# Two norm tiles a unit, their add one step behind, and conjugates ahead of the products

## The chip, the cores and the metric

The kernel runs on one core of one Trainium2 chip. The metric is the device time of the program in microseconds (us); a run's profile also gives the span of the program's instructions on the core. The engines go on independently, each in the order in which its instructions were written, and wait for each other by semaphores: TensorE (PE; its weight loads PEld), VectorE (DVE), ScalarE (ACT), GpSimd (POOL) and SyncE (SP), which here issues the DMA transfers.

## The reference

The input is x with shape (4, 128, 128, 128): 4 batches, 128 channels, an image of 128 x 128. Two layers follow each other.

The first layer treats the 16384 pixels of a batch as a sequence: an MLP, an input projection, a short causal convolution, a selective scan with 16 states for each of 256 channels, a gate and an output projection. Its output is normalised over 4 groups of channels, passed through silu, and x is added:

```python
g = (g - mu) * lax.rsqrt(var + EPS)
xn = jax.nn.silu(g.reshape(B, C, H, W) * gn_w[None, :, None, None] + gn_b[None, :, None, None])
return xn + x
```

The second layer takes that result as `features`. A group norm, a 1x1 convolution with relu and a mean over the image give, through a softmax, four weights per batch. These mix four complex filters, and the product of the spectrum with its filtered self is transformed back:

```python
xf = jnp.fft.rfft2(x32, norm='ortho')
wc = (filt_w[..., 0] + 1j * filt_w[..., 1]).astype(jnp.complex64)
filtered = jnp.fft.irfft2(xf[:, None] * wc[None], s=(h, w), norm='ortho')
ff = jnp.fft.rfft2(filtered, norm='ortho')
product = xf[:, None] * ff
weighted = jnp.sum(weights[:, :, None, None, None].astype(product.dtype) * product, axis=1)
out = jnp.fft.irfft2(weighted, s=(h, w), norm='ortho') + residual_weight * x32
```

## The kernel before

The kernel has two blocks, one after the other. `block0` is the first layer, in chunks of 512 pixels, all four batches; it also finishes the norm, the silu and the pooling of batches 0, 1 and 2 while the next batch is scanned (`finish`, called with its own step numbers). The pixels of a normed batch are written to DRAM as `x1`. `block1` is the spectral part for all batches, and it also has to finish batch 3.

**Units and steps of `block1`.** A unit is 8 channels of one batch: 8 images. There are 16 groups of channels times 4 batches, 64 units. Each unit has three blocks, of 3, 3 and 2 images, and the main loop runs one step `t` per block: unit `t // 3`, block `t % 3`. The work of a block is spread over later steps, so that a step holds work of several blocks. In a step the instructions are written in this order:

- at the first step of a unit, on SP: the filters of a channel group that are due (L736, four transfers of 520 KB) and the images of the next unit, `load(n + 1)` (L742, 512 KB);
- `over_h(t)`: PE transforms each image along its rows into the single PSUM bank `pa` (L776), ScalarE copies half of it to `sa` (L778);
- `evict(t - 8)`: VectorE moves `pz` from PSUM to `sz` (L835);
- `residual(t - 9)`: VectorE adds the last transform in `po` to the image times the residual weight (L848); after a unit's last block SP stores the result (L851);
- `products(t - 2)`: VectorE forms the real and imaginary part of the squared spectrum (L801, L802), then its two products with the mixed filter `wb` (L808, twice);
- `conjugates(t)`: VectorE fills the other half of `sa` from the same bank `pa` (L783);
- `over_w(t - 1)`: PE transforms `sa` into `px` (L790, L791; two banks), ScalarE makes a doubled copy and two squares of it, called xs below (L793 to L795);
- `back_h(t - 7)` and `back_w(t - 8)`: PE transforms back into `pz` (L829, L830; two banks) and `po` (L841; one bank);
- by `t % 3`: the filters of a unit times the batch's weights on ScalarE (`term`, L749: the fourth of this unit at the first step, the first two of the next unit at the second, its third at the third), their sum on POOL (`mix`, L755), on POOL the sums of the products (L815, L816), on ScalarE the mirrored halves (`copies`, L821, L822);
- last, the work of batch 3 that is due in this step, by the phases `pe`, `act`, `dve` and `end`.

The first term of a unit goes into the tile `wb`, of which there are two. It can be written only when the products of the unit two before it have been formed, the last of them in the second step of a unit.

**Batch 3.** `finish` returns a list of (step, phase, function). A norm tile is 512 pixels of all 128 channels; there are 32. `norm_load` issues two loads of 256 KB on SP (L561, L562); `norm_act` is the silu on ScalarE into the PSUM bank `pf` (L567), of which there is one; `norm_dve` adds x on VectorE (L571) and stores the tile to DRAM from SP (L572); `norm_stats` takes the statistics of the second norm on VectorE (L575). The function `norm` gives the steps of load, silu and add: for tile i they are 5 + i, 8 + i and 8 + i. After the last tile come the group statistics, then 32 pooling tiles, one a step (`agg_load`, `agg_mm` L597, `agg_act` L601), from step t1 = 54, then the softmax. The tags `xr` and `o` have four buffers each.

**The order of the units.** Units of batch 3 can't start before its weights are there. `spare` is the last step of `finish` in units; the groups of channels in `wait` are run for batches 0 to 2 first. Of these groups the last three keep their filters for batch 3; the others (`late`) load them once more for a single unit. Before the change `spare` is 33, there are 11 groups in `wait`, 8 of them late, and 5 groups with all four batches in a row.

**Names of stages.** Below, the norm stage is the steps with norm tiles (9 to 40 by the transforms), then a transition, the pooling stage (54 to 85), and the plain stage from 86 to the last step, 191.

Of the kernel before, what the change touches and what calls it, by code (L numbers as in the profile page):

```python
# [500 lines left out]
def group_norm(s, io, b, mat, which, stat, at, then):  # L501


    nc = s.nc
    g = {}

    def small(n, m=1):
        g[n] = io.small.tile([P, m], F32, tag=n, name=f"{n}_{which}_{b}")
        return g[n]

    def aggregate():
        nc.vector.bn_aggr(small("mv", 2), stat().rearrange("p n q -> p (n q)"))

    def mean_mm():
        ps = g["ps"] = io.psum(f"gm_{which}_{b}")
        nc.tensor.matmul(ps[:, 0:1], mat, g["mv"][:, 0:1], start=True, stop=True)

    def spread_act():
        mv = g["mv"]
        nc.scalar.copy(small("mean"), g["ps"][:, 0:1])  # L520
        q = small("q")
        nc.scalar.activation(q, mv[:, 0:1], AF.Square, scale=-1.0, bias=g["mean"])
        nc.scalar.activation(q, q, AF.Identity, bias=mv[:, 1:2])

    def var_mm():
        ps = g["ps"] = io.psum(f"gv_{which}_{b}")
        nc.tensor.matmul(ps[:, 0:1], mat, g["q"], start=True, stop=True)

    def root_act():
        nc.scalar.activation(small("rstd"), g["ps"][:, 0:1], AF.Sqrt, bias=s.eps)  # L530

    def invert():
        nc.vector.reciprocal(g["rstd"], g["rstd"])
        then(g["mean"], g["rstd"])

    return [
        (at, "dve", aggregate), (at, "end", mean_mm), (at + 1, "act", spread_act), (at + 3, "pe", var_mm),
        (at + 3, "act", root_act), (at + 3, "dve", invert),
    ]


def finish(s, io, b, first, norm, agg):

    nc, NCH, C, L, NF = s.nc, s.NCH, s.C, s.L, s.NF
# [86 lines left out]
    todo = group_norm(s, io, b, s.g0, 0, lambda: stats[b], first, start)  # L633
    for i in range(NCH):
        at = norm(i)
        todo += [
            (at[0], "pe", partial(norm_load, i)), (at[1], "act", partial(norm_act, i)),
            (at[2], "dve", partial(norm_dve, i)), (at[2], "end", partial(norm_stats, i)),
        ]
    c = at[2] + 5  # L640
    todo += group_norm(s, io, b, s.g1, 1, lambda: g["stat"], c, middle)
# [1 line left out]
    for i in range(NCH):  # L643
        at = agg(i)
# [11 lines left out]
def block1(tc, s):  # L656
# [7 lines left out]
    nc, B, C, H, W, WF, NF, NCH = s.nc, s.B, s.C, s.H, s.W, s.WF, s.NF, s.NCH  # L664
    HH = H // 2
    filt = s.a["filt_w"].rearrange("f c h w q -> h f c (w q)")
    with ExitStack() as ctx:
        def pool(name, bufs, **kw):
            return ctx.enter_context(tc.tile_pool(name=name, bufs=bufs, **kw))
# [10 lines left out]
        def const(name, shape):  # L680
# [14 lines left out]
        io = SimpleNamespace(  # L695
            big=pool("big", 4), bufs=4, small=small, psum=lambda n: psf.tile([P, T], F32, tag="pf", name=f"pf_{n}")
        )
        t1 = 8 + NCH + 14
        todo = defaultdict(list)
        steps = finish(s, io, B - 1, 0, lambda i: (5 + i, 8 + i, 8 + i), lambda i: (t1 + i - 3, t1 + i, t1 + i, None))  # L700
        for at, phase, f in steps:
            todo[at, phase].append(f)
        spare = max(at for at, _ in todo) // 3 + 2
# [23 lines left out]
        for k, ft in enumerate(spans):  # L727
            at = ft.first - 4
            if k >= KEEP:
                at = max(at, spans[k - KEEP].last)  # L730
            loads[max(at, 0)].append(ft)

        def load_filter(ft):
            ft.t = p2.tile([H, NF, CC, 2 * WF], F32, tag="ft", name=f"ft_{ft.first}", bufs=KEEP)
            for f in range(NF):
                nc.sync.dma_start(out=ft.t[:, f], in_=filt[:, f, ft.c0 : ft.c0 + CC, :])  # L736

        def load(n):
            if n < N:
                c0, b = units[n]  # L740
                u[n].xt = p2.tile([H, CC, W], F32, tag="xt1", name=f"xt1_{n}", bufs=6)
                nc.sync.dma_start(out=u[n].xt, in_=s.x1[b][c0 : c0 + CC].rearrange("c h w -> h c w"))  # L742

        def term(n, f):

            if 0 <= n < N:
                tag, bufs = ("term", 3) if f else ("wb", 2)
                t = p2.tile([H, CC, 2 * WF], F32, tag=tag, name=f"{tag}_{n}_{f}", bufs=bufs)
                nc.scalar.activation(t, u[n].ft.t[:, f], AF.Copy, scale=s.wts[units[n][1]][0:H, f : f + 1])  # L749
                u[n].terms = [t] if f == 0 else u[n].terms + [t]  # L750

        def mix(n, f):
            if 0 <= n < N:
                wb = u[n].terms[0]
                nc.gpsimd.tensor_tensor(wb, wb, u[n].terms[f], ALU.add)  # L755
# [16 lines left out]
        @block  # L772
        def over_h(e, n, m, k):
            e.pa = psa.tile([W, 3, 2, WF], F32, tag="pa", name=f"pa_{n}_{m}")
            for q in range(k):
                nc.tensor.matmul(images(e.pa)[:, q], u[n].xt[:, m + q, :], fh, start=True, stop=True)  # L776
            e.sa = p2.tile([W, 3, 2, H], F32, tag="sa", name=f"sa_{n}_{m}")
            nc.scalar.copy(e.sa[:, 0:k, :, 0:HH], e.pa[:, 0:k, :, 0:HH])  # L778

        @block  # L780
        def conjugates(e, n, m, k):
            o = e.sa[:, 0:k, :, HH:]
            nc.vector.tensor_tensor(o, e.pa[:, 0:k, :, 1:], sign.to_broadcast([W, k, 2, HH]), ALU.mult)  # L783
# [13 lines left out]
        @block  # L797
        def products(e, n, m, k):

            sq = psr.tile([H, 2, 3, WF], F32, tag="sq", name=f"sq_{n}_{m}")  # L800
            nc.vector.tensor_tensor(sq[:, 1, 0:k], e.px[:, 0:k, 0], e.xs[:, 1, 0:k], ALU.mult)  # L801
            nc.vector.tensor_tensor(sq[:, 0, 0:k], e.xs[:, 0, 0:k], e.px[:, 0:k, 1], ALU.subtract)  # L802
            if m == 0:
                u[n].p = [p2.tile([H, 2, CC, WF], F32, tag=f"pr{q}", name=f"pr{q}_{n}") for q in range(2)]
            wv = u[n].terms[0].rearrange("h c (k q) -> h q c k", q=2)
            for q in range(2):
                w = wv[:, q : q + 1, m : m + k, :].to_broadcast([H, 2, k, WF])
                nc.vector.tensor_tensor(u[n].p[q][:, :, m : m + k, :], sq[:, :, 0:k], w, ALU.mult)  # L808
# [23 lines left out]
        @block  # L832
        def evict(e, n, m, k):
            e.sz = p2.tile([W, 3, H], F32, tag="sz", name=f"sz_{n}_{m}")
            nc.vector.tensor_copy(e.sz[:, 0:k], e.pz[:, 0:k])  # L835

        @block
        def back_w(e, n, m, k):
            e.po = pso.tile([H, 3, W], F32, tag="po", name=f"po_{n}_{m}")
            for q in range(k):  # L840
                nc.tensor.matmul(e.po[:, q, :], e.sz[:, q, :], iw, start=True, stop=True)  # L841

        @block
        def residual(e, n, m, k):
            if m == 0:
                u[n].ot = p2.tile([H, CC, W], F32, tag="ot", name=f"ot_{n}")
            o, xt = u[n].ot[:, m : m + k], u[n].xt[:, m : m + k]
            nc.vector.scalar_tensor_tensor(o, xt, s.resw[0:H], e.po[:, 0:k], ALU.mult, ALU.add)  # L848
            if m + k == CC:
                c0, b = units[n]  # L850
                nc.sync.dma_start(out=s.out[b, c0 : c0 + CC].rearrange("c h w -> h c w"), in_=u[n].ot)  # L851

        with tc.manual_schedule():
            load(0)
            for t in range(3 * N + LAG + 3):
                n, i = divmod(t, 3)
                if i == 0:
                    for ft in loads[n]:
                        load_filter(ft)
                    load(n + 1)  # L860
                    if n == 0:
                        for f in range(NF):
                            term(0, f)
                            if f:
                                mix(0, f)
                over_h(t)
                evict(t - LAG - 1)
                residual(t - LAG - 2)
                products(t - 2)
                conjugates(t)  # L870
                over_w(t - 1)
                back_h(t - LAG)
                back_w(t - LAG - 1)
                if i == 0:
                    if n:
                        term(n, 3)
                        mix(n, 2)
                    copies(n - 2)
                elif i == 1:
                    term(n + 1, 0)  # L880
                    term(n + 1, 1)
                    if n:
                        mix(n, 3)
                else:
                    term(n + 1, 2)
                    sums(n - 1)
                    mix(n + 1, 1)
                for phase in ("pe", "act", "dve", "end"):
                    for f in todo[t, phase]:
                        f()  # L890
# [79 lines left out]
```

## Time and profile before

| | us |
|---|---|
| median of 3 runs | 7444.82 (7441.77 to 7446.32) |
| the profiled execution | 7446.74 |
| its span | 7445.0 |
| second block's first transform starts | 6626.55 |
| norm stage, first transform of step 9 to that of step 41 | 184.9 |
| transition, to step 54 | 49.9 |
| pooling stage, to step 86 | 141.7 |
| plain stage, to the transform of step 191 | 378.3 |

In the profile an engine's busy time is the union of its instructions. A line of instructions has start, duration, engine, source line, operation, output and inputs, their shapes and a count, and in brackets the idle time of the engine ahead of it with what ended it. A line of waits has the waiting instruction, the one that it waited for, the sum, the count and the longest. "Granted clock" is the share of its full clock that TensorE was given.

### The profile page before, as it was taken

The page shows a single profiled execution, that of the slowest core. Times are in us where ns is not written, and L with a number is a line of the kernel's source. Part 1 is how long each engine was busy: PE and PEld are TensorE (multiplying, and loading weights), DVE is VectorE, ACT ScalarE, POOL GpSimd, SP SyncE. Part 2 cuts the span into 40 slices and gives each one's busy share as a digit, 9 for nine tenths or more (in the row PEclk, how much of TensorE's full clock was granted, in tenths as well). Part 3 has the DMA queues.
Part 4 walks back from the last instruction along what each step waited for, and adds up shares of the span by engine and source line. Part 5 has one row for each costly group of instructions (what it writes and reads, how often), then busy time and mean ns, then how long its engine had stood idle before and what let it go on. Part 6 is the DMA issues. An engine that isn't in the chain of part 4 may idle for free.

```text
span 7445.0 us, 90541 instructions
## 1 busy us (share of the span) xinstructions
PE 6005.7 (81%) x25908; PEld 2664.1 (36%) x25908; DVE 7031.4 (94%) x8168; ACT 6328.6 (85%) x13181; POOL 6900.6 (93%) x3188
## 2 busy tenths in 40 slices
PE   7787878877778788887777788877777788867999
PEld 2223223322222233332222223232222233237999
DVE  6999999999999999999999999999999999977787
ACT  6888888888888888888888888888888888866887
POOL 6999999999999999999999999999999999976788
PEclk8888888888888888888888889988888889889999
DMA  4444444444554544544545454445554554547665
GB/s 138 159 154 150 151 156 156 143 161 168 174 188 164 179 165 156 169 166 169 184 168 185 161 171 166 159 165 175 171 188 166 173 169 151 173 149 216 177 185 155
DMA packets 853767, 1242.06 MB, mean 167 GB/s; under 512 B 76680, under 2 KB 308240, under 8 KB 853264
## 3 DMA queue, kind: packets, MB, share of 16 engines
q1 hardware_dynamic: 851152, 1236.11, 50.3%
q8 instruction: 204, 3.34, 0.2%
q14 instruction: 299, 2.45, 0.1%
q10 hardware_dynamic: 2112, 0.16, 0.0%
HBM read 992.71 MB, written 243.27 MB: 166 GB/s over the span
## 4 chain that ended last, share of the span: by engine, by line
ACT 20%; DVE 19%; PE 17%; POOL 9%; issue 8%; DMA 5%; SPq 1%; DVEq 0%; ACTq 0%; POOLq 0%
DVE da L409 8%; ACT da L391 8%; DVE h L409 6%; PE pp_cv L231 5%; ACT bt L299 4%; POOL hb L358 4%; POOL hb L416 4%; DVE hb L411 3%; DMA dd<-delta 2%; PE y L430 2%; PE pa L776 1%; ACT L391 1%; PE px L790 1%; PE px L791 1%; POOL du L307 1%
## 5 line engine op out<-in xcount | busy, mean ns | idle before, releaser
L358 POOL TENSOR_TENSOR hb<-rdu,rB 128x1536 f32<-128x1536 f32 (+2 forms) x1536 | 3607.6, 2365 | 16.2 <-DMA rdu<-dd 16.2
L416 POOL TENSOR_TENSOR hb<-h,rC 128x1024 f32<-128x1024 f32 (+1 forms) x1072 | 2438.7, 2277 | 279.8 <-DVE h L409 263.0
L391 ACT ACTIVATE da<-rdelta,amat 128x512 f32<-128x512 f32 x4096 | 2674.6, 696 | 9.2 <-ACT st L412 0.2
L409 DVE TENSOR_TENSOR_SCAN da<-da,st,hb 128x512 f32<-128x512 f32 x1976 | 2420.3, 1268 | 7.1 <-ACT da L391 7.0
L378 PE MATMUL b<-ident,bt 128*128 128x128 f32 x4096 | 768.9, 311 | 767.9 <-DVE h L409 633.0
L430 PE MATMUL y<-hb,sel 128*32 128x512 f32 x8192 | 1364.0, 743 | 4.8 <-POOL hb L416 2.9
L409 DVE TENSOR_TENSOR_SCAN h<-da,st,b 128x512 f32<-128x512 f32 x992 | 1261.3, 1271 | 111.4 <-POOL hb L358 37.5
L411 DVE TENSOR_TENSOR hb<-da,rC 128x512 f32<-128x512 f32 x2040 | 1296.7, 674 | 3.0
L409 DVE TENSOR_TENSOR_SCAN h<-da,st,hb 128x512 f32<-128x512 f32 x1000 | 1252.7, 1256 | 1.3 <-ACT da L391 1.3
L299 ACT ACTIVATE bt<-pt_dut,xdt 128x256 f32<-128x256 f32 x2048 | 1194.6, 708 | 46.8 <-PE pt_dut L288 46.5
L231 PE MATMUL pp_cv<-xm,wck 128*128 128x512 f32 x2048 | 1111.7, 692 | 9.8 <-ACT zs L225 9.7
L378 PEld LDWEIGHTS b<-ident,bt 128*128 128x128 f32 x4096 | 532.0, 156 | 1341.4 <-DVE h L409 997.1
L412 ACT COPY st<-da 128x1 f32<-128x1 f32 x2040 | 295.8, 173 | 567.9 <-DVE hb L411 562.6
L231 PEld LDWEIGHTS pp_cv<-xm,wck 128*128 128x128 f32 x2048 | 438.4, 226 | 771.1 <-issue 502.8
L755 POOL TENSOR_TENSOR wb<-wb,term 128x1040 f32<-128x1040 f32 x192 | 460.9, 2401 | 157.2 <-ACT term L749 147.2
L288 PE MATMUL pt_dut<-ident,du 128*128 128x128 f32 x1024 | 214.1, 337 | 280.5 <-ACT st L412 271.4
L426 PE MATMUL y<-u,diag 128*128 128x512 f32 x512 | 291.0, 651 | 156.8 <-DVE zs L440 155.6
L307 POOL TENSOR_TENSOR du<-delta,u 128x512 f32<-128x512 f32 x256 | 319.0, 1267 | 37.5 <-ACT delta L270 37.5
L417 ACT COPY st<-h 128x2 f32<-128x2 f32 (+1 forms) x1072 | 214.7, 200 | 162.8 <-DVE h L409 154.6
L288 PEld LDWEIGHTS pt_dut<-ident,du 128*128 128x128 f32 x1024 | 134.1, 164 | 578.6 <-POOL du L307 419.2
L196 PE MATMUL pp_h<-xt,w 128*128 128x512 f32 x512 | 296.6, 707 | 51.7 <-DMA xt<-in_x 46.6
L391 ACT ACT_TABLE_LOAD x261 | 334.9, 1283 | 2.9
(137 smaller groups left out, 8019.0 us busy)
## 6 DMA issues: line engine op xcount, KB each, us to landing
rdelta<-dd SPq DMA_DIRECT2D x1024, 256.0 KB, 3.6
rdu<-dd SPq DMA_DIRECT2D x1024, 256.0 KB, 4.6
rC<-bc SPq DMA_DIRECT2D x512, 256.0 KB, 5.1
rB<-bc SPq DMA_DIRECT2D x384, 256.0 KB, 3.5
dd<-delta SPq DMA_DIRECT2D x256, 256.0 KB, 5.3
dd<-du SPq DMA_DIRECT2D x256, 256.0 KB, 4.5
ft<-in_filt_w SPq DMA_DIRECT2D x96, 520.0 KB, 7.1
xt<-in_x SPq DMA_DIRECT2D x128, 256.0 KB, 5.5
```

The source lines that it names most:

```text
L231: nc.tensor.matmul(ps["cv", j], w, d["xm"][:, t : t + T], start=t == 0, stop=t == KC - 1)
L288: nc.tensor.transpose(ps["dut"][:, 2 * t + j, :], d["du"][:, j, at : at + P], s.ident)
L299: nc.scalar.activation(d["bt"][:, 2 * h + t, :, :, q], src, AF.Copy, scale=d["xdt"][:, 2 * h + t, R + q : R + q + 1])
L307: nc.gpsimd.tensor_tensor(du, d["delta"][:, j, :], d["u"][:, j, :], ALU.mult)
L358: nc.gpsimd.tensor_tensor(hb[:, p : p + n, :], d["du", j][:, m : m + n, :], d["B"][:, p - 1 : p - 1 + n, :], ALU.mult)
L378: nc.tensor.transpose(b[:, t * P : (t + 1) * P], src, s.ident)
L391: nc.scalar.activation(d["da", p][q], d["delta", j][:, m, :], AF.Exp, scale=s.amat[:, c : c + 1])
L409: nc.vector.tensor_tensor_scan(o, das[q], b, init, ALU.mult, ALU.add)
L411: nc.vector.tensor_tensor(hb[:, p + q, :], das[q], d["C"][:, p + q, :], ALU.mult)
L416: nc.gpsimd.tensor_tensor(hb[:, ps, :], h[:, q, :], d["C"][:, ps, :], ALU.mult)
L430: nc.tensor.matmul(y[m * DG : (m + 1) * DG, :], s.sel, d["hb", j, r][:, p, :], start=False, stop=r == NG - 1)
L755: nc.gpsimd.tensor_tensor(wb, wb, u[n].terms[f], ALU.add)
```

## The change

Three edits, all of them in the second block. In a step, VectorE's conjugates of block `t` are written ahead of the products of block `t - 2`. The add of a norm tile gets a phase of its own, "add", which is written right behind the products and in front of the column transform; it belongs to the step after its silu's. The statistics stay in the phase "end", at the step of the add. And the tiles come two in a unit instead of three: the silu of tile i at step 9 + 3 (i // 2) + i % 2, its load three steps ahead, its add one step behind. The last silu is thus at step 55 and its add at 56; `t1` becomes 70, `spare` 38, and `wait` has 13 groups, 10 of them late, with 3 groups of four batches in a row. For batches 0 to 2 `finish` keeps its default, "dve".

```diff
-def finish(s, io, b, first, norm, agg):
+def finish(s, io, b, first, norm, agg, add="dve"):
...
-            (at[2], "dve", partial(norm_dve, i)), (at[2], "end", partial(norm_stats, i)),
+            (at[2], add, partial(norm_dve, i)), (at[2], "end", partial(norm_stats, i)),
...
-        t1 = 8 + NCH + 14
+
+        def norm(i):
+            t = 9 + 3 * (i // 2) + i % 2
+            return t - 3, t, t + 1
+
+        t1 = norm(NCH - 1)[2] + 14
         todo = defaultdict(list)
-        steps = finish(s, io, B - 1, 0, lambda i: (5 + i, 8 + i, 8 + i), lambda i: (t1 + i - 3, t1 + i, t1 + i, None))
+        steps = finish(s, io, B - 1, 0, norm, lambda i: (t1 + i - 3, t1 + i, t1 + i, None), "add")
...
                 residual(t - LAG - 2)
+                conjugates(t)
                 products(t - 2)
-                conjugates(t)
+                for f in todo[t, "add"]:
+                    f()
                 over_w(t - 1)
```

## The prediction

> **What bounds the kernel now.** First the page, for the whole:
>
> ```profile
> span 7445.0 us, 90541 instructions
> PE 6005.7 (81%) x25908; PEld 2664.1 (36%) x25908; DVE 7031.4 (94%) x8168; ACT 6328.6 (85%) x13181; POOL 6900.6 (93%) x3188
> ```
> These shares average over two blocks; the change touches only the second, from about 6627 us on. So next its stages, cut at the first transform of step 9 (6666.26), 41 (6851.16), 54 (6901.10) and at 86 (7042.77). Columns: stretch, length, busy time (count) of PE, PEld, DVE, ACT, POOL, granted clock, DMA share, GB/s.
>
> ```profile
> 6666.26:6851.16 184.90, 138.29 (x1025) 130.48 (x1023) 134.60 (x289) 117.14 (x226) 103.60 (x54) 0.92 0.72 220
> 6851.16:6901.10 49.94, 48.29 (x424) 47.79 (x425) 40.10 (x95) 41.81 (x86) 43.52 (x24) 1.00 0.70 186
> 6905.00:7037.00 132.00, 132.00 (x1017) 117.97 (x1016) 90.68 (x210) 107.48 (x240) 96.90 (x50) 1.00 0.66 185
> 7070.00:7420.00 350.00, 349.89 (x3114) 349.48 (x3114) 289.97 (x683) 286.85 (x587) 314.19 (x162) 1.00 0.66 175
> ```
> In the last two PE is busy all the time: it sets the pace, 10.78 us a unit of three steps in the plain stage. In the first, the norm stage, nobody is full: 32 steps take 184.9 us, 17.33 us a unit. The waits of 6640 to 6880 us say why (us in total, times, longest):
>
> ```profile
> DVE of L571 <- ACT pf_n L567: 47.2, 21, 4.1
> ...
> PE pa L776 <- DVE sa L783: 35.8, 30, 2.6
> ```
> and the timeline shows one turn of that wait:
>
> ```profile
> 6763.37 0.76 DVE L808 TENSOR_TENSOR pr<-sq,wb 128x260 f32<-128x260 f32 x2
> 6764.05 0.55 DVE L783 TENSOR_TENSOR sa<-pa,c_sign 128x384 f32<-128x384 f32 x1
> 6764.17 1.16 ACT L749 ACTIVATE wb<-ft,wts 128x1040 f32<-128x1040 f32 x1 [1.31 <-DVE pr L808]
> ...
> 6765.24 1.15 ACT L749 ACTIVATE term<-ft,wts 128x1040 f32<-128x1040 f32 x1
> ...
> 6766.29 0.76 ACT L567 ACTIVATE pf_n<-of,bias,scale 128x512 f32<-128x512 f32 x1
> ...
> 6767.08 0.69 DVE L571 TENSOR_TENSOR of<-pf_n,xr 128x512 f32<-128x512 f32 x1 [2.48 <-ACT pf_n L567]
> ```
> ScalarE's first term needs the buffer that the products release; two terms and the silu follow; VectorE, with all else queued behind the add, stands 2.48 us. Round one unit by hand, with the intervals listed below: 2.95 from the products' end to this add; add, stats, evict, residual, products, conjugates 4.26 to the next; from these conjugates 5.6 to the third add (transform 0.95, column transform 1.15, xs 0.66, term 1.05, y copies 1.02, silu 0.77); 3.66 to the products' end. That is 16.5. The trace has 16.4 and 17.9 in turn, the longer where the clock is halved (six transform matmuls in 1.67 us rather than 0.94). The hand method holds, so I use it for the new order.
>
> **What the Trainium skill says.** "PSUM — Partial Sum Buffer", section "PSUM bank collisions raise a hardware error": two engines must not be in one bank at once, reads included. The trace agrees: ScalarE's copy and VectorE's conjugates read the same bank, and each of the 192 conjugates starts at least 0.03 us after its copy ends. Brought forward, they can't overtake the copy. "TensorE: Matmul & The Clock Gate", Part 1: the clock halves after an idle window; the trace has 0.92 in the norm stage and 1.00 after. "DMA: Bandwidth & Descriptors", section "Queues, rings and completion order": each DMA engine takes descriptors in ring order. In the trace an image load (xt) behind a filter load lands 11.8 to 13.5 us after the filter's first issue, against some 5 alone.
>
> **The change, part by part.** Intervals start to start, from this timeline, for three-image (two-image) blocks: evict 0.46 (0.38), residual 0.53 (0.39), conjugates 0.46 (0.33), products 0.39+0.40+0.95 = 1.74 (0.32+0.33+0.69 = 1.34, 1.41 to their end), add 0.73, stats 0.61. ScalarE: copy 0.48 (0.36), xs about 0.8, term 1.05, two y copies 1.02, silu 0.70.
>
> *Two tiles a unit.* 32 tiles take 16 units, 48 steps, instead of 32 steps. The total stays 64 units, so 16 steps leave the plain stage: 378.3 us from step 86 to 191 in 105 steps is 3.60 each, 57.6 us. The transition (49.9 us, 13 steps) and the 32 pooling steps keep their lengths. Break-even for a norm unit: (184.9 + 57.6) / 16 = 15.2 us.
>
> *The new norm unit.* VectorE alone: two blocks of 3.19 and one of 2.4, 8.8 us, and two tiles of 1.34: 11.5 us. The chain is longer. From the two-image conjugates: 0.33, products 1.74, add and stats of the odd tile 1.34, evict and residual 0.99, conjugates 0.46, products 1.74, evict 0.38, residual 0.53, conjugates 0.46, products to their end 1.41: 9.38. Then ScalarE: 0.04, two terms 2.11, silu of the odd tile 0.70, copy 0.36, 0.03, and the conjugates again: 3.24. Sum 12.62. In that last leg VectorE has only add, stats, evict and residual (2.2 us), so it stands about 1.1 us: this is where the removed wait goes. The add itself no longer waits, its silu being a step old; the even add frees the PSUM bank for the odd silu while the terms run. PE needs 10.8; ScalarE 287/350 of 10.78 and two silus, 10.2; POOL 314/350, 9.7: none is nearer.
>
> *Transfers.* A norm tile moves 0.79 MB; a unit 2 x 0.79 + 0.52 in + 0.52 out + a third of a 2.13 MB filter = 3.3 MB. The packets' own times in this stage (347 GB/s for 2 KB, 281 for 512 B, 254 for the filter's 520 B) make it 4.5 + 3.7 + 2.8 = 11.1 us of the 16 engines: 88% of 12.6. It fits, but bursts. SP is in order, and the store of the odd tile now holds it until that add ends, 2.8 us after the two-image conjugates. Filters and xt issue behind it, at 3.2; xt lands 12.1 later, at 15.3; the transform that reads it could start at 13.05. Now this load has about 4 us in hand. The image transform is thus 2.3 late; VectorE is busy until 17.0 anyway, but xs, term, copies, silu follow late and the next conjugates start 1.2 us late. That is every third unit, 5.3 x 1.2 = 6 us. The tile loads, three steps ahead, now reuse a buffer two steps after its store, not one, which loosens the old wait. Their issues move with them past SP's filters, but land at about 19 with silu at 20.5.
>
> *Clock.* Halved stretches cost the old stage some 0.7 us a unit (17.33 - 16.5, rounded down). PE's idle gaps shrink from a quarter to 15%; I keep 0.2 a unit, 3 us; bounds 0 and 0.7.
>
> Norm stage: 16 x 12.62 + 6 + 3 = 211 us.
>
> *Conjugates forward, in the PE-bound stages.* They now wait for the copy with nothing between. Worst step: copy ends 7246.33, conjugates to 6.82, products to 8.25 instead of 6.64; ScalarE's term starts 8.29 instead of 7.58, the two-image copy ends 10.76 and conjugates 11.2; PE wants them at 12.14. Hidden by 0.9 us; without that cover each us late would be lost once a unit. The loop of the norm unit, without its odd tile (1.34) and silu (0.70), is 12.62 - 2.04 = 10.58, 0.2 under PE's 10.78: no loss, narrowly. The residual moves 0.2 us later, and with it SP's filter loads; xt lands there 0.1 to 0.9 ahead of use, so some of 13 such units lose 0.1 to 0.2: +2 us (0 to 5).
>
> *More units before the last batch's weights.* The first wait covers 13 channel groups, not 11; two more groups come back as single units, two more filter loads, 4.3 MB. They run under PE, within the +2.
>
> Sum: 211 + 2 - 184.9 - 57.6 = -29.5 on the span of 7445.0, 7415.5; that execution took 7446.74, so 7417 like for like; from the median 7444.82, 7415.
>
> **Rivals.**
> A, the forecast: the terms' leg binds, 7415, chance 0.62; for a unit of 12.0 to 13.9 us in all, 7396 to 7427.
> B, transfers or an unseen wait bind: the old stage moved 220 GB/s with stalls on stores in its chain; 3.3 MB at 230 is 14.4 us, 16 x 14.4 = 230, change -10: 7435. For it: filter stretches of 97% DMA share. Against: 260 GB/s in just those. 0.16.
> C, VectorE alone binds, with the terms hidden better than I think: 11.6 x 16 = 186, -54: 7391. Against it: the buffer that the products release is the only one free. 0.11.
> D, slower: the conjugates' wait for the copy joins the loop of the plain stage. The slack is 0.2 us; about 35 units (30 plain, 5 of transition) pay what exceeds it. A loop of 11.7 eats the 30 us; one of 12.1, that is the wait of some 0.5 in all three steps, gives +46 - 30: 7461. For it: VectorE's 290 of 350 busy leaves it 1.8 us a unit. Against: VectorE already stands 0.99 and 0.48 us there for PE, which absorbs a later start. 0.11.
> That nothing happens is excluded: the step numbers change for every tile.
>
> **The numbers.** No change can be told within 0.2%, 15 us: 7430 to 7460. Faster: A, C and a quarter of B: 0.77. Same: the rest of B and a little of D, 0.14. Slower 0.09. The range takes A, most of B and the near end of C, 7396 to 7440; A's own is 7396 to 7427.
>
> **What would show it.** Right: adds without wait behind silu; the conjugates of two-image blocks standing about 1 us for ScalarE's copy in the norm stage; tiles two a unit at 12.6 to 13.2; a late image load in every third unit; pooling and plain stages with PE full at 13.3 and 10.8. Wrong: a plain unit above 10.9 (D); POOL or DMA ending VectorE's waits in the norm stage (B); the stage under 190 us (C).

## The result, and the profile after

The changed kernel takes 7430.44 us (median of 22 runs, 7422.93 to 7438.14) against 7440.71 for the kernel before (22 runs beside it, 7431.76 to 7446.32). The ratio is 0.9986, with a 95% interval of 0.9980 to 0.9992: 10 us less, a real difference by the interval, but inside the 0.2% that the prediction took for the least that can be told. The forecast was 29.5 us less.

The page of the changed kernel, span and engines:

```profile
span 7429.0 us, 90286 instructions
PE 5999.6 (81%) x25908; PEld 2658.5 (36%) x25908; DVE 7023.0 (95%) x8168; ACT 6329.1 (85%) x13181; POOL 6905.3 (93%) x3188
```

Its stages, cut at the first transform of steps 9, 57, 70 and 102 and at that of step 191; columns as before (stretch, length, busy time and count of PE, PEld, DVE, ACT and POOL, granted clock, DMA share, GB/s):

```profile
6667.19:6875.90 208.71, 182.69 (x1538) 177.17 (x1536) 179.45 (x399) 164.66 (x322) 155.99 (x81) 0.98 0.79 240
6875.90:6927.23 51.33, 47.58 (x418) 47.01 (x419) 40.89 (x97) 41.34 (x86) 41.89 (x22) 1.00 0.58 159
6927.23:7069.49 142.26, 142.26 (x1094) 126.97 (x1093) 96.09 (x228) 116.18 (x256) 105.59 (x56) 1.00 0.70 197
7069.49:7405.13 335.64, 323.37 (x2849) 321.92 (x2848) 260.57 (x628) 263.34 (x541) 286.15 (x147) 0.99 0.65 173
```

The last line is the surprise: before, PE was busy for 349.89 of 350 us of the plain stage; now 12.3 of 335.64 us are idle, in a stage that was meant to lose steps and keep its pace.

| stage of the second block, us | before | after | forecast of the difference | measured |
|---|---|---|---|---|
| start, to step 9 | 39.7 | 41.6 | 0 | +1.9 |
| norm stage | 184.9 | 208.7 | +26.1 (211) | +23.8 |
| transition, 13 steps | 49.9 | 51.3 | 0 | +1.4 |
| pooling, 32 steps | 141.7 | 142.3 | 0 | +0.6 |
| plain stage to step 191 | 378.3 | 335.6 | -55.6 | -42.7 |
| sum | | | -29.5 | -15.0 |

So the profiled executions differ by 15 us in these stages, and the medians of 22 runs by 10. The first block is not touched, yet its end lies anywhere from 6621.9 to 6630.3 us in the profiled executions of this study; the stages are therefore compared by their own lengths.

**The norm stage came as forecast.** Its waits (total, times, longest):

```profile
DVE sa L788 <- ACT sa L783: 25.2, 23, 2.1
...
PE pa L781 <- DMA xt<-x: 10.2, 5, 2.7
```

The wait of the add for its silu, 47.2 us before, is not in that list any more. In its place VectorE's conjugates (now L788) wait for ScalarE's copy. The timeline of one unit, first ScalarE, then VectorE:

```profile
6715.49 1.16 ACT L754 ACTIVATE wb<-ft,wts 128x1040 f32<-128x1040 f32 x1 [0.20 <-DVE pr L813]
6716.56 1.15 ACT L754 ACTIVATE term<-ft,wts 128x1040 f32<-128x1040 f32 x1
6717.62 0.76 ACT L567 ACTIVATE pf_n<-of,bias,scale 128x512 f32<-128x512 f32 x1
6718.32 0.36 ACT L783 COPY sa<-pa 128x256 f32<-128x256 f32 x1
...
6717.16 0.47 DVE L853 SCALAR_TENSOR_TENSOR ot<-xt,resw,po 128x256 f32<-128x256 f32 x1
6718.71 0.42 DVE L788 TENSOR_TENSOR sa<-pa,c_sign 128x256 f32<-128x256 f32 x1 [1.08 <-ACT sa L783]
```

Two terms, the silu of the odd tile, the copy of two images, then the conjugates, which stood 1.08 us where 1.1 was worked out. The five waits for an image, 10.2 us, are the late image of the filter units.

**The plain stage has three late spots.** Its units take 10.7 to 11.2 us, but for 14.7 and 12.4 (units 45 and 46), 14.2 (unit 52), and 15.5 and 12.3 (units 59 and 60). Here is the first spot, with lines of ScalarE, SP, PE and ScalarE:

```profile
7191.12 1.15 ACT L754 ACTIVATE term<-ft,wts 128x1040 f32<-128x1040 f32 x1
...
7192.29 3.63 SPq L741 DMA_DIRECT2D ft<-in_filt_w  x4
7196.03 1.64 SPq L747 DMA_DIRECT2D xt<-x  x1
...
7203.41 0.91 PE L781 MATMUL pa<-c_fh,xt 128*128 128x130 f32 x4 [3.84 <-DMA xt<-x]
...
7204.80 0.48 ACT L783 COPY sa<-pa 128x384 f32<-128x384 f32 x1 [4.83 <-PE pa L781]
```

Unit 45 begins on PE at 7188.69. In the other filter units of this stage SP issues the filters 2.2 to 2.8 us ahead of the unit's start; here it does so 3.6 us behind it, at 7192.29, just when the last term of unit 45 has ended (7191.12 + 1.15 = 7192.27). The image for unit 46 stands behind these filters in SP's order. It lands at 7203.28, and PE, done with its work before at 7199.57, starts at 7203.41. From its issue this image took 7.25 us, the three before it, each behind filters too, 6.6 to 6.9: it was not carried much more slowly, it was issued late. SP's own waits in this stage name the same term, three of them 6.1 us long; the kernel before has no such wait in its plain stage:

```profile
SPq L741 <- ACT term L754: 19.2, 4, 6.1
```

The code says why that term. A filter has four buffers (KEEP), and a load is put at the unit `max(first - 4, last use of the buffer)`. With the old grouping `first - 4` was always the later of the two, by three units or more, so the buffer had long been free. With 13 groups in `wait`, three groups of four batches remain, followed by 3, 3 and 4 single units, and for three loads the two are equal, at units 45, 52 and 59: these loads are put at the start of the very unit that reads the buffer last, ahead of its fourth term. SP waits there for that term, and all behind it waits too.

### The profile page after: what moved, and what is told of

It is laid out like the page before. It is cut to its first block, busy times and chain, and to the rows that moved or that the text cites. A ratio compares the mean times of both kernels' runs of the same rounds, so it can differ in the third digit from the quotient of the medians.

```text
span 7429.0 us, 90286 instructions
## 1 busy us (share of the span) xinstructions
PE 5999.6 (81%) x25908; PEld 2658.5 (36%) x25908; DVE 7023.0 (95%) x8168; ACT 6329.1 (85%) x13181; POOL 6905.3 (93%) x3188
## 4 chain that ended last, share of the span: by engine, by line
DVE 21%; ACT 19%; PE 15%; issue 8%; POOL 8%; DMA 5%; SPq 1%; DVEq 0%; ACTq 0%; POOLq 0%
DVE da L409 9%; ACT da L391 8%; DVE h L409 6%; PE pp_cv L231 5%; ACT bt L299 4%; POOL hb L416 3%; POOL hb L358 3%; DVE hb L411 3%; DMA dd<-delta 2%; PE y L430 2%; ACT L391 1%; POOL du L307 1%; PE pa L781 1%; SPq L315 1%; PE po L846 1%
```

## The experiments

Stage lengths below are those of each run's profiled execution. "Before" is the kernel before, run beside it on the same chip.

**Theory.** The forecast's chain for the norm stage holds; the missing 15 us are SP standing for a filter buffer, three times, with the image behind it. **Rivals.** The DMA engines can't carry three or four filters in a row (bandwidth); or the conjugates' new place slows the plain stage (rival D of the prediction).

**The grouping alone (e3_groups).**

```diff
-        spare = max(at for at, _ in todo) // 3 + 2
+        spare = 38
```

> The kernel before with one edit: spare = 38, so 13 channel groups wait for the last batch and three groups remain with single units three, three and four in a row, as in the changed kernel; order on VectorE and norm tiles as before. Theory (the rearranged units make SP wait for a filter buffer still in use, three times): the norm stage stays at 185 us, and the plain stage has three late units; 13 to 17 us slower than before. Rival (the late units come from the conjugates' new place or from the shorter norm stage): no difference from before, within 4 us.

Measured: 7464.45 us against 7444.98, ratio 1.0027 (1.0017 to 1.0038), 19 us slower. Norm stage 184.6; plain stage 397.9 instead of 378.3, with units of 14.5 and 13.3, 14.6 and 12.4, 15.6 and 12.9. The wait for the image in its plain stage:

```profile
PE pa L776 <- DMA xt<-x: 12.7, 4, 4.6
```

and SP's wait for the term:

```profile
SPq L736 <- ACT term L749: 18.9, 4, 6.2
```

In the changed kernel's plain stage the wait for the image reads:

```profile
PE pa L781 <- DMA xt<-x: 12.0, 4, 4.6
```

The late units come with the grouping, without conjugates or tiles moved. Rival D falls as their cause.

**The buffer free by a unit (e5_free_buffer).** The changed kernel, with

```diff
-                at = max(at, spans[k - KEEP].last)
+                at = max(at, spans[k - KEEP].last + 1)
```

> The changed kernel with one edit: a filter load is put one unit later where its buffer is still read by the unit that runs (last + 1 instead of last); it moves three loads by a unit. Theory (SP stands for that buffer, 3 to 4 us, three times, and the image load behind it is late): the three stalled spots go, 13 to 16 us less than the changed kernel, 23 to 26 less than before; the norm stage stays at 209. Rival (bandwidth: four filters in a row are more than the DMA engines carry): moving three loads one unit later leaves most of the stall, under 5 us won.

Measured: 7417.98 against 7444.98, ratio 0.9964 (0.9951 to 0.9978): 27 us less than before. The plain stage falls from 335.6 to 322.2, 13.4 us; no unit is above 11.5; norm stage 208.2. The same wait is now:

```profile
PE pa L781 <- DMA xt<-x: 1.1, 3, 0.5
```

Three loads are moved by one unit, and all bytes and groups are kept. SP's wait for the term is gone from this stage. The move also spreads loads that stood in consecutive units; the next run leaves them there.

**The image ahead of the filters (e4_image_first).** The changed kernel, with

```diff
+                    load(n + 1)
                     for ft in loads[n]:
                         load_filter(ft)
-                    load(n + 1)
```

> The changed kernel with one edit: at a unit's start SP issues the image load of the next unit ahead of the filters. Theory (the image is late only because it stands behind the filters in SP's order): the three stalled spots of the plain stage go, 15 us, and the late image in every third norm unit too, 8 to 11 us: 23 to 26 us less than the changed kernel, 33 to 36 less than before. Rival (the DMA engines are short of bandwidth where filters follow each other): then whichever comes second is late, terms wait for filters, and less than half of that is won.

Measured: 7411.92 against 7444.98, ratio 0.9956 (0.9943 to 0.9968): 33 us less. Plain stage 318.7, 10.74 a unit, with PE full (first line) though SP still stands for the term (second line):

```profile
7061.45:7380.19 318.74, 318.66 (x2849) 318.25 (x2848) 259.60 (x628) 263.76 (x541) 286.31 (x147) 1.00 0.68 182
SPq L741 <- ACT term L754: 16.2, 4, 5.5
```

The filters are issued in the same units as in the changed kernel, and no engine waits for them: the bandwidth was not short there, and SP's stand costs time only through the image behind it. Norm stage 203.1, with fifteen units in a row (4 to 18) at 12.7 us: the image that was late in every third unit cost 208.7 - 203.1 = 5.6 us (forecast 6), not the 8 to 11 of this run's expectation. And 12.7 is the chain's 12.62. PE's clock in 140 us of that stage is 1.00 (the line after: stretch, length, busy times, clock, DMA share, GB/s):

```profile
6700.00:6840.00 140.00, 124.32 (x1063) 120.13 (x1062) 124.19 (x277) 113.08 (x222) 107.43 (x56) 1.00 0.87 265
```

**The image ahead of the filters in the kernel before (e12_before_image_first).** The same edit in the old kernel.

> The kernel before with the image load ahead of the filters and nothing else. There the image has about 4 us in hand in the norm stage and 0.1 to 0.9 in the plain stage's filter units, so little is to be won: norm stage 185 as before, plain stage 1 to 3 us shorter; 0 to 4 us less than before. If the edit helps whatever the order of the units, 15 us or more less than before.

Measured: 7442.22 against 7442.99, ratio 1.0000 (0.9992 to 1.0008). Plain stage 377.7 instead of 378.3. The norm stage was 181.4 instead of 184.9; its units are again 16.4 or 17.8 to 18.0, with fewer of the long ones (the granted clock of the stage is 0.94, before 0.92); but the start took 42.8 us instead of 39.7. The edit is worth some 23 us in the changed kernel (33 of e4 less the 10 of the change) because of what the change made late.

**The conjugates alone (e1_conj).** The kernel before, with

```diff
-                products(t - 2)
                 conjugates(t)
+                products(t - 2)
```

> The kernel before with one edit: conjugates written ahead of the products; three tiles a unit and the add in its old place. By the chain of the prediction the norm unit keeps its 2.95 us stand at the add behind the two terms and loses the 1.0 us stand at the first step's add, because the transform is released 1.7 us earlier: about 1 us a unit, 10.7 units, so 8 to 12 us less than before, all of it in the norm stage. Plain and pooling units stay at 10.8 and 13.3. If bringing the conjugates forward costs the plain stage (the slower rival of the prediction), plain units rise above 10.9.

Measured: 7448.34 against 7444.98, ratio 1.0002 (0.9994 to 1.0011): nothing won. Norm stage 181.7, 3.2 less; start 2.1 and transition 2.1 more; plain 10.84 a unit. The expectation had the transform released by the conjugates. In the trace it is not: on PE it is queued behind the back transform of the step before, which waits for the residual, and the residual is queued on VectorE behind the add. VectorE and then PE of one unit:

```profile
6772.20 0.69 DVE L571 TENSOR_TENSOR of<-pf_n,xr 128x512 f32<-128x512 f32 x1 [2.96 <-ACT pf_n L567]
...
6773.99 0.47 DVE L848 SCALAR_TENSOR_TENSOR ot<-xt,resw,po 128x256 f32<-128x256 f32 x1
...
6774.52 1.59 PE L841 MATMUL po<-c_iw,sz 128*128 128x128 f32 x6 [3.07 <-DVE ot L848]
6775.90 1.51 PE L776 MATMUL pa<-c_fh,xt 128*128 128x130 f32 x6
```

As long as the add waits for a silu of its own step, the rest of the step stands with it, wherever the conjugates are.

**The conjugates put back (e6_no_conj).** The changed kernel with products ahead of conjugates again, the add still behind both.

> The changed kernel with one part undone: products ahead of the conjugates again. By the chain, the two terms and the odd silu (3.2 us) then lie beside conjugates, add, stats, evict, residual and products (4.4 us), so VectorE doesn't stand for the copy, and the norm unit is VectorE's own 11.5 to 12.0 us instead of 12.7 where no image is late; late images every third unit stay, and grow with the shorter unit. Norm stage 190 to 203 instead of 209, and about 2 us each less in the start and the transition; the plain stage keeps its three late units: 8 to 22 us less than the changed kernel. Rival (the forward conjugates are part of what makes the norm stage short): norm stage 215 or more, slower than the changed kernel.

Measured: 7411.92 against 7443.49, ratio 0.9958 (0.9946 to 0.9971): 32 us less than before, so about 21 less than the changed kernel. Norm stage 188.6 instead of 208.7, start 39.7 instead of 41.6, transition 50.2 instead of 51.3; the plain stage keeps its three late spots (338.4). The late images of the norm stage, expected to stay and grow, nearly went: 1.6 us in 2 waits, where the changed kernel has 10.2 in 5. Of the three edits this one costs time, once the add is moved: with the conjugates behind the products, VectorE has 4.4 us of work beside the terms, the silu and the copy, and with them ahead only 2.2.

**Three tiles a unit (e2_three).** The changed kernel with `t = 9 + i` in `norm`.

> The changed kernel with one part undone: three norm tiles a unit (silu of tile i at step 9 + i), with the add still one step behind and the conjugates ahead. The chain of the prediction gets a third add and statistics, 12.6 + 1.3 = 14.0 us a unit, and the transfers of three tiles are 13.3 us of the DMA engines a unit, so 14.0 to 15.0: 32 steps in 149 to 160 us instead of 185 before. The units are ordered as before (spare 33), so no unit stands for a filter buffer: 20 to 34 us less than before, that is 10 to 20 less than the changed kernel. If two tiles a unit are what makes the norm stage short (the add a step behind alone isn't enough), the unit stays at 16 to 17 and the time at that of before.

Measured: 7438.10 against 7443.49, ratio 0.9992 (0.9984 to 1.0001). Norm stage 173.7 for 33 steps, 15.8 a unit: better than 17.3, short of the 14 to 15 expected; and the time is 5 us less than before where 20 to 34 were expected. Units without a filter load are at 12.8 to 15.3, those with one at 17.4 to 22.1. The image is late in most units:

```profile
PE pa L781 <- DMA xt<-x: 35.3, 8, 10.8
```

**Three tiles with the image ahead (e8_three_image_first).** The edit of e4 added.

> The changed kernel with three norm tiles a unit and the image load ahead of the filters. In the run with three tiles alone the units with filters took 17 to 22 us and the others 14 to 15, with SP standing for stores to land ahead of the tile loads. If the image is late in the filter units only because of its place behind the filters, those fall to 14 to 15.5: norm stage 150 to 158 instead of 174, 16 to 24 us less than three tiles alone. If the DMA engines (13.3 us of transfers a unit) or SP's stand for the stores is the limit, the stage stays over 162, and the image is still waited for.

Measured: 7434.99 against 7442.99, ratio 0.9990 (0.9983 to 0.9996). The first expectation fails: norm stage 176.0, with three units of 19.6 to 23.1 still, each right behind the issue of a filter. Other waits take the place of the one removed; the last line is SP's own wait, for a tile's store to land before the buffer is loaded again:

```profile
ACT pf_n L567 <- DMA of<-ob: 15.3, 3, 7.5
PE pa L781 <- DMA xt<-x: 15.2, 5, 3.9
SPq L562 <- DMA x<-of: 74.6, 28, 4.3
```

Three tiles need 4.1 MB a unit, at 13.3 us of the DMA engines; the stage moves 240 GB/s at a share of 0.81. Whether the engines' rate in bursts or SP's stand for stores is the last cause I did not separate. The stand comes with these step numbers: a tile has one of four buffers, and here the load of tile i + 4 falls in the very step of tile i's add and store. In the kernel before it falls one step later (36.5 us of this wait in the norm stage), in the changed kernel two steps later, and there the wait is absent. So these two runs don't show that three tiles a unit can't do as well: three tiles with later loads or a fifth buffer, and three tiles with the products ahead of the conjugates, were not run. Nor were two tiles with the add in its old place.

**A third buffer for the first term (e9_wb3_image_first).** The kernel of e4, with

```diff
-                tag, bufs = ("term", 3) if f else ("wb", 2)
+                tag, bufs = ("term", 3) if f else ("wb", 3)
```

> The changed kernel with the image load ahead of the filters (which alone gave a norm unit of 12.7 and 7412 us) and a third buffer for the tile wb. If the leg from the products' end over two terms and the odd silu to the copy sets the 12.7 us, as the prediction has it, the terms no longer wait for the products and the unit falls to VectorE's own 11.5 to 11.9: 12 to 18 us less than with the image load alone. If the 12.7 come from something else (transfers, the clock), it stays within 3 us of that.

Measured: 7388.58 against 7443.49, ratio 0.9927 (0.9915 to 0.9940). Norm stage 186.6, 11.6 a unit.

**The conjugates put back and the image ahead (e10_no_conj_image_first).**

> The changed kernel with the image load ahead of the filters and the products ahead of the conjugates again. If VectorE's stand for the copy is what the forward conjugates cost in the norm stage: norm unit 11.5 to 12.0, stage 184 to 192 instead of 203, start and transition 2 us shorter each, plain stage at 10.75 a unit: 7390 to 7400. If transfers (11.1 us of the DMA engines a unit) set it instead, the unit stays over 12.2.

Measured: 7391.40 against 7443.49, ratio 0.9929 (0.9917 to 0.9941). Norm stage 185.2, 11.5 a unit; plain 319.7. Its norm stage in the same 140 us as above, followed by that of the third buffer:

```profile
6700.00:6840.00 140.00, 133.90 (x1173) 131.61 (x1172) 135.82 (x305) 123.47 (x242) 118.32 (x62) 1.00 0.96 293
```
```profile
6700.00:6840.00 140.00, 132.49 (x1160) 130.21 (x1159) 135.51 (x303) 122.67 (x244) 117.24 (x61) 1.00 0.95 289
```

VectorE is busy for 135.8 and 135.5 of 140 us, where e4 had 124.2. Beside the image's place, the two edits have nothing in common but the leg "products, two terms, silu, copy, conjugates", and each brings the unit to 11.5 or 11.6 us, VectorE's own 11.5: that leg was the limit. Both versions beat the kernel before by 52 to 55 us and so the changed one by 42 to 45; which of the two is faster these runs don't tell.

## Why the prediction was right or wrong

The time fell in the stated range (7396 to 7440) and on the stated side, but outside the likeliest case's own range (7396 to 7427), and by the 0.2% bound the outcome is "same", given 0.14. That it lies in the range is luck: the range took in most of rival B, whose reason did not come true.

- *Two tiles a unit, 16 steps out of the plain stage*: right in the step count; what the remaining steps cost is below.
- *The new norm unit, 12.62*: right. With no late image it is 12.7, the stand for the copy 1.08 us for 1.1; both edits that take the leg away give the 11.5 of VectorE alone (11.5 and 11.6).
- *Transfers in the norm stage, 6 us*: right, 5.6 measured; with the image issued first the DMA engines were no limit at 12.6 a unit, nor with a share of 0.96 at 11.5.
- *Clock, 3 us*: the granted clock in the stage is 0.98, and the stage came 2 us under the forecast; within its bounds.
- *Conjugates forward in the PE-bound stages, no loss*: right for the plain stage (10.84 against 10.81 with that edit alone). Not seen: the start and the transition, 2 us each, where PE is not full.
- *"More units before the last batch's weights ... run under PE, within the +2"*: this step failed, and it is nearly the whole difference. The two more filter loads were counted as bytes; the step did not follow where the loads are put. In the plain stage 89 steps at 3.60 are 320.6 us; it took 335.6, 15.0 more instead of 2. What stood there was SP, 6.1 us each time, for a filter buffer still in use, with the image behind it. The grouping alone costs the old kernel 19 us, and putting the three loads a unit later gives 13.4 us back; what is left, 322.2, is 1.6 above 320.6, near the +2.

Rival B, that transfers or an unseen wait bind, has the right total (-10) by luck: its sum was for transfers in the norm stage, which kept its forecast; the unseen wait was in the plain stage, and bandwidth was not its cause. The sign set down for rival D, a plain unit above 10.9, appeared (up to 15.5) although D was not the cause: e3 has the same units without the conjugates moved. I had not asked what the bound in one line of `loads` could do, since that line was not in the diff; what feeds it was.

## What to carry to other kernels

When a change shifts a count that a planner uses (here the number of groups), work the planner through with the new count: which load meets which buffer, and what stands behind it in the issuing queue. On an in-order queue issue what is needed next ahead of what is needed in four units; here that won some 23 us where the image had become late, and nothing in the kernel before. And when a wait is moved, look for the work that lies beside it in its new place: the conjugates ahead of the products left 2.2 us of cover for a leg of 3.2, behind them 4.4.

## What I had not expected of the hardware

With the conjugates put back and the image ahead (e10), the DMA engines carried 293 GB/s over 140 us with a share of 0.96, nearly all in packets of 512 B, 520 B and 2 KB, and PE, VectorE, ScalarE and GpSimd never waited for a transfer in it; the forecast, at 88%, had feared bursts.
